# Two repeated operands of a selective scan, moved from shared tiles into tiles of their own

## The chip, the cores and the metric

The kernel runs on one core of one Trainium2 chip. The metric is the device time of one execution in microseconds (us); lower is better. All arithmetic is fp32. The core has five instruction streams that matter here: PE (matrix products), DVE (vector), ACT (activation functions), POOL (GpSimd, elementwise here) and SP, which computes nothing and issues nearly all DMAs.

## The reference, cut to what matters

The network has two layers. Layer 0 normalizes an image batch (4, 384, 32, 32) over channels, runs a selective scan over its 1024 pixels in four directions, adds the residual, and sends the tokens through a top-2-of-4 mixture of experts. Layer 1 is an attention whose query, key and value are one projection, followed by a factored feed-forward. The change lies in the scan:

```python
dts = jnp.einsum('bkrl,kdr->bkdl', dts, dt_projs_weight)
dt = jax.nn.softplus(dts + dt_projs_bias[None, :, :, None])
def step(h, inp):
    dtt, ut, bt, ct = inp
    dA = jnp.exp(dtt[..., None] * A)
    h = h * dA + (dtt * ut)[..., None] * bt[:, :, None, :]
    y = jnp.einsum('bkdn,bkn->bkd', h, ct)
    return (h, y)
```

There are 4 images, 4 directions k, 384 channels d, and 16 states n for each channel. dt and dt * u have no state axis, so a kernel that lays states on partitions has to repeat them over the states.

## The kernel before, in words

**Tiling of the scan.** A unit is one image, one direction and one half of the pixels (HF = 512); there are 4 x 4 x 2 = 32 units, in the order of `scan_layer` (L235 to L240). A unit is worked in three chunks of 128 channels (`chunk`, L373), so the scan has 96 chunks. The 128 partitions of a tile in a chunk hold 4 states x 32 channels, so a chunk needs 4 groups of states (g, NG = 4) times 4 blocks of 32 channels. The blocks are taken in two pairs: q = 0 and q = 1, each with j = 0 and 1.

**What one chunk does.** First it loads, for each q, a tile `dtr` of 128 x 2 x 2 x 512 (8 KB a partition, L382): index s = 0 is dt, s = 1 is dt * u, and each is repeated over the four states, so it is filled by eight DMAs of 128 KB out of the scratch array `dd` in HBM (L386). The pool holds three such tiles (`bufs=3`), and one chunk uses two. Then, for each g and each q:

- POOL multiplies dt * u by B into a tile `bx` of 128 x 1024 (L401; six buffers);
- ACT makes `da` = exp(A * dt) in PSUM, one instruction for each j (L410; two buffers);
- DVE runs the recurrence over 512 pixels, one `tensor_tensor_scan` for each j (L415). For q = 0 the result goes into `bx`, for q = 1 into `da`;
- the product with C is POOL's for q = 0 (L429, 128 x 1024) and DVE's for q = 1 (L422, 128 x 512, one for each j);
- PE sums over the states into `acc` (L436), which frees `bx`. After four groups DVE adds `acc` to the image's result (L276 or L280).

So a chunk holds 8 POOL products of L401 and 4 of L429, 16 exponentials, 16 scans, and 16 matmuls. In units that begin a direction, a DVE copy keeps the last column (L421, L426) as the carry for the next unit.

**What makes dt.** `project` (L287) runs for the next unit while this unit is scanned; `next(project)` (L267) advances it one step for each g. For each c of three it makes dt by softplus out of six ACT instructions (`begin`, L343 to L348), two POOL subtractions (L360, L361), two DVE instructions (L366, L367) and an ACT copy (L368), and stores dt and dt * u to `dd` (L369, L370). Its temporaries come from one tag, `k2`, of 2 KB tiles with seven buffers: `wdt` and `xd`, which live through the whole of `project`, and for each c `mag`, `one_e` and `lnw`. `mag` and `one_e` are what the stores read, so their buffers come free when the stores have landed. `k2` also serves the squares of `layernorm` (L159) and the residual tiles of `finish` (L228).

**What sets the order.** Each engine and SP work through a queue of their own, in order. The order in each queue is made when the program is built, by the framework's scheduler, out of a timing model of its own; buffers are handed out there too, so a change of tile sizes can move instructions on every queue. `issue_after` (L351) keeps the POOL and DVE steps of `project` behind named steps of the chunk.

**What runs beside the scan.** The later stages of image b (routing, experts, attention and feed-forward, called the tail here) are worked beside the scan of the images after it; the experts' weights come in 576 KB DMAs on the same SP queue (L740, L748). The last image's experts, attention and feed-forward come after the end of the scan. Attention loads its projection weights in four pieces of 128 columns into the tag `got` (L863, 1.5 KB), which has two buffers in the room `NARROW` (the tail beside the scan) and three in `WIDE` (the last image).

Of the kernel before, what the change touches and what calls it, by code (L numbers as in the profile page):

```python
# [9 lines left out]
F32 = mybir.dt.float32  # L10
I32 = mybir.dt.int32
AF = mybir.ActivationFunctionType
# [5 lines left out]
P = 128  # L18
# [5 lines left out]
HF = 512  # L24
# [20 lines left out]
DB = 32  # L45
NB = D // DB
NJ = P // DB
# [21 lines left out]

NARROW = {"kw": 8, "k12": 2, "k4": 4, "got": 2, "bb": 2}
WIDE = {"kw": 11, "k12": 3, "k4": 4, "got": 3, "bb": 2}
EXACT = {"kw": 4, "k12": 2, "k4": 4, "got": 2}

# [33 lines left out]
class Body:  # L109
# [34 lines left out]
    def layernorm(self, src, dst, eps, psum, work):  # L144

        nc = self.nc
        for i in range(NH):
            sl = halves(i)
            mean = psum.tile([P, HF], F32, tag="ps", name="ln_mean")
            for c in range(DC):  # L150
                nc.tensor.matmul(mean, self.ones, src[:, c, sl], start=(c == 0), stop=(c == DC - 1))
            for c in range(DC):
                nc.vector.scalar_tensor_tensor(
                    dst[:, c, sl], mean, -1.0 / D, src[:, c, sl], op0=ALU.mult, op1=ALU.add
                )

            sqs = []
            for c in range(DC):
                sq = work.tile([P, HF], F32, tag="k2", name="ln_sq", bufs=7)  # L159
                nc.scalar.activation(sq, dst[:, c, sl], AF.Square)  # L160
                sqs.append(sq)
            nm = HF // P
            var = psum.tile([P, HF], F32, tag="ps", name="ln_var")
            for m in range(nm):
                for c in range(DC):
                    nc.tensor.matmul(
                        var[:, m : m + 1], sqs[c][:, m * P : (m + 1) * P], self.ones[:, :1],
                        start=(c == 0), stop=(c == DC - 1),
                    )
            std = work.tile([P, nm], F32, tag="ln_std", name="ln_std", bufs=2)  # L170
            self.exp_again(
                nc.scalar.activation(std, var[:, :nm], AF.Sqrt, bias=eps, scale=1.0 / D).ins
            )
            nc.vector.reciprocal(std, std)
            rows = psum.tile([P, HF], F32, tag="ps", name="ln_rows")
            for m in range(nm):
                nc.tensor.matmul(
                    rows[:, m * P : (m + 1) * P], std[:, m : m + 1].to_broadcast([P, P]),
                    self.ident, start=True, stop=True,
                )  # L180
            for c in range(DC):
                nc.vector.tensor_mul(dst[:, c, sl], dst[:, c, sl], rows)
# [3 lines left out]
    def scan_layer(self, x1, between):  # L186

        nc, tc, a = self.nc, self.tc, self.a
        with ExitStack() as ctx:
            wp = ctx.enter_context(tc.tile_pool(name="s_w", bufs=1))  # L190
            work = ctx.enter_context(tc.tile_pool(name="s_work", bufs=1))
# [6 lines left out]
            nega = wp.tile([P, KG * NB * NG], F32, tag="nega", name="nega")  # L198
# [20 lines left out]
            def finish(b, y):  # L219
                self.layernorm(y, y, self.eps5, psum, work)  # L220
                for c in range(DC):
                    ins = nc.scalar.activation(
                        y[:, c, :], y[:, c, :], AF.Gelu,
                        bias=self.col("lnb", c), scale=self.col("lnw", c),
                    ).ins
                    rows = slice(c * P, (c + 1) * P)
                    for i in range(NH):
                        x = work.tile([P, HF], F32, tag="k2", name="x", bufs=7)  # L228
                        nc.sync.dma_start(out=x, in_=a["x"][b][rows, halves(i)])
                        nc.gpsimd.tensor_add(x, x, y[:, c, halves(i)])  # L230
                        nc.sync.dma_start(out=x1[b][rows, halves(i)], in_=x)
                self.exp_again(ins)
# [15 lines left out]
            for n, unit in enumerate(units):  # L248
# [13 lines left out]
                for c in range(DC):  # L262
# [5 lines left out]
                    if k % 2 == 0:  # L268
                        ys = y[:, c, halves(i)]
                        out = acc  # L270
# [16 lines left out]
    def project(self, unit, u, wx, work, dram, psum, made):  # L287

        nc, a = self.nc, self.a
        b, k, i = unit
        by_cols = k % 2 == 1
        w = slice(i * (HW // NH), (i + 1) * (HW // NH))

        def part(c):
            if by_cols:
                return u[:, c, :].rearrange("p (h w) -> p w h", h=HW)[:, w, :]
            return u[:, c, halves(i)]  # L300

        def split(ap):
            return ap.rearrange("p (w h) -> p w h", h=HW) if by_cols else ap

        def k2(name, shape=(P, HF)):
            return work.tile([*shape], F32, tag="k2", name=name, bufs=7)

        wdt = k2("wdt", (R, D))
        nc.sync.dma_start(out=wdt, in_=a["wdt"][:, k, :])
        ps = psum.tile([P, HF], F32, tag="ps", name="xd_ps")  # L310
        for c in range(DC):
            nc.tensor.matmul(  # L312
                split(ps[:XD, :]), wx[:, c, k, :], part(c), start=(c == 0), stop=(c == DC - 1)
            )
        xd = k2("xd", (XD, HF))
        nc.scalar.copy(xd, ps[:XD, :])
        rows = dram.tile([2 * NS, HF], F32, tag="rows", name="rows")
        nc.sync.dma_start(out=rows, in_=xd[R:XD, :])
        view = rows.rearrange("(t g n) l -> n t g l", t=2, g=NG)
        bcs = []  # L320
        for h in range(NG // 2):
            bc = work.tile([P, 2, 2, HF], F32, tag="bcs", name="bcs", bufs=3)
            for n in range(NJ):
                for t in range(2):
                    nc.sync.dma_start(
                        out=bc[n * DB : (n + 1) * DB, t],
                        in_=view[n, t, 2 * h : 2 * h + 2].partition_broadcast(DB),
                    )
            bcs.append(bc)

        dd = dram.tile([2, D, HF], F32, tag="dd", name="dd")
        made += [bcs, dd]
        yield

        def begin(c):
            ps = psum.tile([P, HF], F32, tag="ps", name="dt_ps")
            nc.tensor.matmul(ps, wdt[:, c * P : (c + 1) * P], xd[:R, :], start=True, stop=True)  # L340
            bias = self.col("dtb", k * DC + c)
            mag, one_e, lnw = k2("mag"), k2("one_e"), k2("lnw")
            nc.scalar.activation(mag, ps, AF.Abs, bias=bias)  # L343
            nc.scalar.activation(ps, ps, AF.Relu, bias=bias)
            nc.scalar.activation(mag, mag, AF.Exp, scale=-1.0)
            nc.scalar.activation(one_e, mag, AF.Identity, bias=1.0)
            nc.scalar.activation(lnw, one_e, AF.Ln)
            nc.scalar.activation(one_e, one_e, AF.Identity, bias=self.minus1)  # L348
            return ps, mag, one_e, lnw

        def behind(engine):  # L351
            if self.place_behind is None:
                return nullcontext()
            return self.tc.issue_after(self.place_behind[engine])

        for c in range(DC):
            ps, mag, one_e, lnw = begin(c)
            yield
            with behind("pool"):
                nc.gpsimd.tensor_sub(mag, one_e, mag)  # L360
                nc.gpsimd.tensor_sub(lnw, lnw, mag)  # L361
            yield
            d, du = mag, one_e
            rows = slice(c * P, (c + 1) * P)
            with behind("dve"):
                nc.vector.tensor_add(ps, ps, lnw)  # L366
                nc.vector.tensor_mul(split(du), split(ps), part(c))  # L367
            nc.scalar.copy(d, ps)  # L368
            nc.sync.dma_start(out=dd[0, rows, :], in_=d)  # L369
            ins = nc.sync.dma_start(out=dd[1, rows, :], in_=du).ins  # L370
        made.append(ins)

    def chunk(self, unit, first, c, fed, carry, nega, sel, acc, work, dap):  # L373
# [5 lines left out]
        bcs, dd, _ = fed  # L379
        dtr = []  # L380
        for q in range(NJ // 2):
            t = work.tile([P, 2, 2, HF], F32, tag="dtr", name="dtr", bufs=3)  # L382
            at = c * P + q * 2 * DB
            for n in range(NJ):
                for s in range(2):
                    nc.sync.dma_start(  # L386
                        out=t[n * DB : (n + 1) * DB, s],
                        in_=dd[s, at : at + 2 * DB, :].rearrange("(j d) l -> d j l", d=DB),
                    )
            dtr.append(t)  # L390

        def run(ap):
            return ap[:, ::-1] if k >= 2 else ap
# [2 lines left out]
        for g in range(NG):  # L396
            bc = bcs[g // 2]
            out = []
            for q in range(NJ // 2):
                bx = work.tile([P, 2, HF], F32, tag="bx", name="bx", bufs=6)  # L400
                pool = nc.gpsimd.tensor_mul(  # L401
                    bx, dtr[q][:, 1], bc[:, 0, g % 2].unsqueeze(1).to_broadcast([P, 2, HF])
                ).ins
                cg = bc[:, 1, g % 2]
                at = ((c * 2 + q) * NG + g) * 2
                for j in range(2):
# [1 line left out]
                    col = (k * NB + block) * NG + g  # L408
                    da = dap.tile([P, HF], F32, tag="da", name="da")
                    nc.scalar.activation(  # L410
                        da, dtr[q][:, 0, j, :], AF.Exp, scale=nega[:, col : col + 1]
                    )
                    hold = carry[:, at + j : at + j + 1]
                    h = bx[:, j, :] if q == 0 else da
# [877 lines left out]
```

## Time and profile before

| | |
|---|---|
| median of 3 runs | 4843.51 us (4836.32 to 4863.11) |
| profiled execution | 4820.35 us, its span 4816.9 us |
| POOL busy | 3095.1 us (64%) |
| DVE busy | 3038.3 us (63%) |
| PE busy | 3556.8 us (74%) |
| ACT busy | 2563.6 us (53%) |
| mean granted TensorE clock | 0.813 |

The span is the time between the first and the last instruction of the profiled execution; the 3.45 us between it and the execution's own time lie around the program. Busy shares are means over the whole span, and the kernel has two stages: the scan, up to about 3617 us, and what is left of the last image's tail, to the end. In the stretch from 60 to 1000 us POOL is busy for 855.04 of 940 us, from 2000 to 3000 us for 834.19 of 1000 us, and from 3615 us on for 66.74 of 1202 us. A busy share of a stage is therefore what to read, then the idle time of the engine that is fullest there, and what ended it. In the answers about waits, "A <- B: t, n" means that engine A sat idle for t us in all, n times, before the instruction named first, until the one named after the arrow was done.

### The profile page before, as it was taken

What the parts mean: (1) busy time and instruction counts of PE and PEld (TensorE: products, weight loads), DVE (VectorE), ACT (ScalarE), POOL (GpSimd) and SP (SyncE); (2) the same over time, 40 slices, a digit from 0 to 9 for tenths busy, and PEclk for the clock granted to TensorE, in tenths of its full rate; (3) what the DMA queues carried; (4) which work ended last, traced back from release to release, by engine and by line L of the source; (5) the groups of instructions that cost most, each with busy time, mean ns of one, the idle gap of its engine ahead of it and who ended that gap; (6) DMA issues with size and microseconds to landing.
All of it is one profiled execution on the core that took longest, in us unless ns stands there. A gap on an engine that the chain in (4) does not pass through costs nothing. (4 is left out here: it accounts for less than half of the span.)

```text
span 4816.9 us, 46613 instructions
## 1 busy us (share of the span) xinstructions
PE 3556.8 (74%) x13984; PEld 1713.4 (36%) x13984; DVE 3038.3 (63%) x4276; ACT 2563.6 (53%) x4390; POOL 3095.1 (64%) x1515
## 2 busy tenths in 40 slices
PE   4333334479996787566999868865789999998797
PEld 1000002245552222223556512222457665554323
DVE  5888886767778776987877788898772020002101
ACT  4454444455665666464666677655554243343454
POOL 5999997688888678778886889987880110001000
PEclk6555555589997888777999889876899999999797
DMA  4454463388777334346787754434965663332000
GB/s 110 110 118 106 110 159 92 99 238 223 216 221 203 98 96 121 80 131 189 221 242 213 197 144 102 121 88 120 262 181 185 202 226 105 125 105 91 15 15 14
DMA packets 402884, 685.56 MB, mean 142 GB/s; under 512 B 50496, under 2 KB 203456, under 8 KB 402624
## 3 DMA queue, kind: packets, MB, share of 16 engines
q1 hardware_dynamic: 393888, 656.94, 49.2%
q0 software_dynamic: 8192, 25.17, 1.6%
q8 instruction: 112, 1.84, 0.2%
q14 instruction: 148, 1.21, 0.1%
q10 hardware_dynamic: 544, 0.40, 0.0%
HBM read 557.53 MB, written 124.78 MB: 142 GB/s over the span
## 5 line engine op out<-in xcount | busy, mean ns | idle before, releaser
L401 POOL TENSOR_TENSOR bx<-dtr,bcs 128x1024 f32<-128x1024 f32 x768 | 1798.1, 2364 | 287.4 <-PE acc L436 150.9
L410 ACT ACTIVATE da<-dtr,nega 128x512 f32<-128x512 f32 x1536 | 1041.9, 689 | 1172.7 <-DVE bx L422 688.8
L429 POOL TENSOR_TENSOR bx<-bx,bcs 128x1024 f32<-128x1024 f32 x384 | 904.2, 2356 | 156.3 <-DVE carry L426 69.8
L436 PE MATMUL acc<-bx,sel 128*32 128x512 f32 x3072 | 563.9, 770 | 594.0 <-POOL bx L429 468.6
L786 PE MATMUL h_ps<-xc,w 128*128 128x256 f32 x3168 | 770.4, 397 | 67.5 <-DVE xc L770 32.4
L802 PE MATMUL y_ps<-w,hs 128*128 128x384 f32 x2112 | 741.0, 503 | 35.9 <-ACT hs L795 32.0
L786 PEld LDWEIGHTS h_ps<-xc,w 128*128 128x128 f32 x3168 | 614.5, 198 | 269.7 <-issue 97.5
L415 DVE TENSOR_TENSOR_SCAN bx<-da,carry,bx 128x512 f32<-128x512 f32 x384 | 473.9, 1269 | 122.1 <-POOL bx L401 69.8
L802 PEld LDWEIGHTS y_ps<-w,hs 128*128 128x128 f32 x2112 | 404.9, 195 | 368.0 <-issue 85.6
L415 DVE TENSOR_TENSOR_SCAN da<-da,carry,bx 128x512 f32<-128x512 f32 x384 | 475.9, 1273 | 89.5 <-ACT da L410 51.7
L415 DVE TENSOR_TENSOR_SCAN bx<-da,bx 128x512 f32<-128x512 f32 x384 | 453.6, 1210 | 100.4 <-POOL bx L401 62.1
L415 DVE TENSOR_TENSOR_SCAN da<-da,bx 128x512 f32<-128x512 f32 x384 | 454.7, 1218 | 95.5 <-POOL bx L401 53.0
L422 DVE TENSOR_TENSOR bx<-da,bcs 128x512 f32<-128x512 f32 x768 | 507.4, 678 | 2.2
L820 POOL DMA_INDIRECT got<-made,g_pos x64 | 60.7, 948 | 656.6 <-PE s_ps L894 506.1
L899 ACT ACTIVATE ex<-s_ps 128x512 f32<-128x512 f32 x512 | 299.2, 590 | 318.8 <-PE s_ps L894 318.2
L436 PEld LDWEIGHTS acc<-bx,sel 128*32 128x32 f32 x3072 | 76.5, 120 | 967.3 <-POOL bx L429 654.1
L894 PE MATMUL s_ps<-w 64*128 64x512 f32 x1024 | 312.2, 680 | 95.3 <-ACT ex L899 95.2
L791 ACT ACTIVATE hs<-h_ps,bb 128x256 f32<-128x256 f32 x528 | 210.8, 470 | 208.5 <-PE h_ps L786 208.4
L806 DVE TENSOR_TENSOR y<-y_ps,bb 128x384 f32<-128x384 f32 x88 | 48.4, 550 | 427.6 <-PE y_ps L802 426.5
L943 PE MATMUL o_acc<-ex,vt 128*64 128x512 f32 x1024 | 301.1, 667 | 0.0
L340 PE MATMUL dt_ps<-xd,wdt 12*128 12x512 f32 x192 | 141.0, 822 | 66.7 <-ACT mag L368 47.3
L312 PE MATMUL xd_ps<-u,wx 128*44 128x512 f32 x192 | 143.1, 894 | 61.4 <-ACT mag L368 61.4
(182 smaller groups left out, 3743.9 us busy)
## 6 DMA issues: line engine op xcount, KB each, us to landing
w<-in_w SPq DMA_DIRECT2D x352, 576.0 KB
dtr<-dd SPq DMA_DIRECT2D x1536, 128.0 KB
bcs<-rows SPq DMA_DIRECT2D x512, 128.0 KB
dd<-one_e SPq DMA_DIRECT2D x96, 256.0 KB
dd<-mag SPq DMA_DIRECT2D x96, 256.0 KB
rows<-zero SPq DMA_DIRECT2D x88, 192.0 KB
xs<-rows SPq DMA_DIRECT2D x44, 384.0 KB
made<-y SPq DMA_DIRECT2D x44, 384.0 KB
```

Source lines behind the costliest of these rows:

```text
L401: pool = nc.gpsimd.tensor_mul(bx, dtr[q][:, 1], bc[:, 0, g % 2].unsqueeze(1).to_broadcast([P, 2, HF])).ins
L410: nc.scalar.activation(da, dtr[q][:, 0, j, :], AF.Exp, scale=nega[:, col : col + 1])
L415: nc.vector.tensor_tensor_scan(run(h), run(da), run(bx[:, j, :]), 0.0 if first else hold, ALU.mult, ALU.add,)
L422: dve = nc.vector.tensor_mul(bx[:, j, :], h, cg).ins
L429: pool = nc.gpsimd.tensor_mul(bx, bx, cg.unsqueeze(1).to_broadcast([P, 2, HF])).ins
L436: nc.tensor.matmul(acc[lo : lo + DB, :], sel, out[q][:, j, :], start=(g == 0), stop=(g == NG - 1),)
L786: nc.tensor.matmul(ps[:, r, :], w1[(f + r) // wf][:, c, (f + r) % wf * P : ((f + r) % wf + 1) * P], xc[:, c, :], start=(c == 0), stop=(c = ...
L791: nc.scalar.activation(hs[:, f + r, :], ps[:, r, :], AF.Identity, bias=bb[:, f + r : f + r + 1])
L802: nc.tensor.matmul(out[:, :D], hs[:, f, t * P : (t + 1) * P], w2[f // wf][:, f % wf, :], start=(f == 0), stop=(f == FC - 1),)
L894: nc.tensor.matmul(ps[:, o, :], w[rows, j * P : (j + 1) * P], w[rows, halves(i)], start=True, stop=True,)
L899: ins = nc.scalar.activation(ex[:, o, :], ps[:, o, :], AF.Exp, scale=HD**-0.5, accum_out=sums[:, t, 2 * j + o, i : i + 1],).ins
L943: ins = nc.tensor.matmul(out[cols, :], made[t][1][:, j, cols], ex[:, o, :], start=(j == 0), stop=(j == MB - 1),).ins
```

## The change

`dtr` is split: dt and dt * u of one pair q go into two tiles of 128 x 2 x 512 (4 KB a partition) instead of the two halves of one tile of 8 KB. There are seven buffers of 4 KB instead of three of 8 KB: 28 KB instead of 24 KB a partition. The loops over s and n change places, so that the four DMAs of dt are issued before the four of dt * u; their number, sizes and contents stay. Room for the added 4 KB comes from `k2`, six buffers instead of seven (2 KB less), and from `got` in `NARROW`, one instead of two (1.5 KB less). The operations on the data are the same.

```diff
-NARROW = {"kw": 8, "k12": 2, "k4": 4, "got": 2, "bb": 2}
+NARROW = {"kw": 8, "k12": 2, "k4": 4, "got": 1, "bb": 2}
...
-                sq = work.tile([P, HF], F32, tag="k2", name="ln_sq", bufs=7)
+                sq = work.tile([P, HF], F32, tag="k2", name="ln_sq", bufs=6)
...
-                        x = work.tile([P, HF], F32, tag="k2", name="x", bufs=7)
+                        x = work.tile([P, HF], F32, tag="k2", name="x", bufs=6)
...
-            return work.tile([*shape], F32, tag="k2", name=name, bufs=7)
+            return work.tile([*shape], F32, tag="k2", name=name, bufs=6)
...
         for q in range(NJ // 2):
-            t = work.tile([P, 2, 2, HF], F32, tag="dtr", name="dtr", bufs=3)
+
+            pair = []
             at = c * P + q * 2 * DB
-            for n in range(NJ):
-                for s in range(2):
+            for s in range(2):
+                t = work.tile([P, 2, HF], F32, tag="dtr", name="dtr", bufs=7)
+                for n in range(NJ):
                     nc.sync.dma_start(
-                        out=t[n * DB : (n + 1) * DB, s],
+                        out=t[n * DB : (n + 1) * DB],
                         in_=dd[s, at : at + 2 * DB, :].rearrange("(j d) l -> d j l", d=DB),
                     )
-            dtr.append(t)
+                pair.append(t)
+            dtr.append(pair)
...
-                    bx, dtr[q][:, 1], bc[:, 0, g % 2].unsqueeze(1).to_broadcast([P, 2, HF])
+                    bx, dtr[q][1], bc[:, 0, g % 2].unsqueeze(1).to_broadcast([P, 2, HF])
...
-                        da, dtr[q][:, 0, j, :], AF.Exp, scale=nega[:, col : col + 1]
+                        da, dtr[q][0][:, j, :], AF.Exp, scale=nega[:, col : col + 1]
```

Below, L388, L404, L413, L432 and L439 of the kernel after are L386, L401, L410, L429 and L436 of the kernel before; lines up to L370 keep their numbers, and lines from L405 on are three higher.

## The prediction

> **What bounds the kernel now.** I read the stretches first. After 3615 us the scan is over, PE is busy 1088.51 of 1202 us, and the change reaches nothing there directly. Before that no engine is full all the time, so I read the idle time of the fullest one, POOL.
>
> ```profile
> POOL bx L401 <- PE acc L436: 150.9, 28, 35.7
> POOL bx L401 <- DMA dtr<-dd: 113.8, 41, 9.5
> POOL bx L429 <- DVE carry L426: 69.8, 26, 6.6
> POOL mag L360 <- ACT one_e L348: 69.7, 15, 44.4
> POOL bx L429 <- DVE bx L415: 46.9, 23, 3.9
> ```
>
> These are POOL's waits (total us, times, longest us). The second is what the change is about: 113.8 us before L401 until a DMA of `dtr` had landed. One wait of 9.5 us is the start, which stays; 104.3 us in 40 waits are left, 2.6 us each.
>
> The rows by line give POOL's work: L401 768 x 2.364 us, L429 384 x 2.356 us, L360 and L361 96 x (1.272 + 1.275) us. A chunk is 8 x 2.364 + 4 x 2.356 + 2.55 = 30.9 us. The times of the DVE adds that end chunks (L276, L280) show the pace: from 344.79 to 525.65 us six chunks end, 30.1 us each (records of neighbouring instructions overlap a little), so POOL is solid there. With the tail beside the scan, from 828.33 to 3617.39 us, 72 chunks take 38.7 us each: 8 us a chunk lie in a tangle of waits, and the waits for `dtr` are 1.4 us of it (98.8 us of the 104.3 fall here).
>
> Then SP, which issues the loads:
>
> ```profile
> SPq L386 <- ACT da L410: 414.5, 67, 34.9
> ...
> SPq L370 <- DVE one_e L367: 316.1, 54, 21.9
> ...
> SPq L386 <- POOL bx L401: 41.5, 24, 17.8
> ```
>
> A pair's tile is free only when both POOL (dt * u) and ACT (dt) have read it for the last time; ACT is the later one ten times as often by time. ACT is tied to DVE by two `da` buffers:
>
> ```profile
> ACT da L410 <- DVE bx L422: 688.8, 356, 8.8
> ```
>
> POOL runs ahead of both, so it reaches the next chunk's second pair while ACT still holds the tile that this pair's data needs. The order of time shows it, for instance, where three L401 in a row start at 1128.09 after 7.83 us of idle time, released by a load.
>
> **What the Trainium skill says.** "Perfetto Trace Analysis", section Optimization Strategy: the same gap coming again on the engine that should be full can mean that there is no room for the next tile. The trace agrees: 40 gaps, mostly at the second pair of a chunk. "PSUM — Partial Sum Buffer", section Engine vs sequencer instructions: the queues of ScalarE, VectorE and GpSimdE are strictly first in, first out, so an ACT instruction that waits for a store holds the exponentials behind it. Beyond that principle no trace here has such a wait in number. "DMA: Bandwidth & Descriptors", section Anatomy of one DMA, fits 2.0 us plus bytes / 436 GB/s, for the GpSimd path: an estimate of 2.6 us for a 256 KB store. The trace has more on the SP path: a store issued at 50.69 us released ACT at 54.70 us, 4.0 us. I use 4.0.
>
> **The change part by part**, against the profiled 4820.35 us (span 4816.9 + 3.45 around it). The median, 4843.51, is 23.2 us (0.5%) above it; I add the same differences to both.
>
> *1. Seven tiles for three pairs: gain.* A chunk needs four tiles, so three of the next chunk's four can be in place before any tile comes free: both of the first pair, and dt of the second. Only the second pair's dt * u waits for a buffer, and that is the one POOL itself gives back at its last L401 of q = 0, not ACT. At 260 to 280 us, POOL's last such read ends at 268.1 us and ACT's at 269.8; and after it only four issues (about 0.46 us each: 16 took 7.36 us), not eight, have to go out. So it lands about 1.7 + 1.8 = 3.5 us earlier than now. That covers most of 2.6 us a wait; the longest (7.8 us) stay in part. The number of loads is the same (1536 x 128 KB), so SP and HBM do no less work. What is late next: POOL's products with C (L429), which wait for DVE (69.8 + 46.9 us now), because with a busy DVE (80% from 2000 to 3000 us) an earlier `bx` just lies longer. Hence only a share of 104.3 us reaches the end. Bounds: 0 (all handed on) to -104 us; I take half, **-52 us**. The swap of the loops lets ACT start after four loads instead of seven of eight, which helps ACT's 99.5 us of waits for `dtr`; POOL still needs the last of eight. I count it within the half.
>
> *2. The order moves.* In the built program's order, PE has 2885 matmuls after the last `acc` matmul instead of 2951: 66 fewer, half an expert's slot. From 3615 us on PE takes 1088.51 / 4387 = 0.248 us each, so 16 us; they go into the scan, where PE is busy for 80 to 83% and delays `acc` in turn. Bounds 0 to -16; I take **-8 us**. In the first image POOL's order was two products of L401 to one of L429; now it is mostly six, then three. Over three groups POOL needs 23 us, DVE 3 x 6.3 + 1.8 = 20.7 us; but the third L429 waits for five half groups of scans that begin behind the first L401, 16.9 us, against 16.2 to 17.5 us of POOL's own queue. Before, four POOL products (9.4 us) lay between the first product of a group and its L429, against 2.5 us of scans. So DVE's slack falls from about 7 us to under 1 us. At 0 to 1 us for each of some 30 such bursts: 0 to +30, I take **+8 us**. The later images have about the old mixture.
>
> *3. Six `k2` instead of seven: loss.* `wdt` and `xd` hold two, so four are left for three temporaries; the next `lnw` (L347) needs a buffer that a store of the channel block before still reads. In the order of ACT's waits, 83 of 96 L347 now wait for a DMA, where 4 did; of L343 70, where 30 did; L346 falls from 40 to 6. Queued behind on ACT are the exponentials, for which DVE waits, and for DVE POOL's L429. How long a wait is depends on the exponentials between the copy L368 and the wait: with two or fewer (55 waits) 4.0 us of landing against 2 x 0.69 us at the least leaves up to 2.6 us. A `da` that is ready ahead covers about one scan, 1.25 us. Upper bound: 55 x 1.35 = 74 us. But before, 22 such short waits stood in the order, and the trace shows one hold of 2.9 us. Bounds 0 to +74, I take **+10 us**. `layernorm` and `finish` use six at most; hidden.
>
> *4. One `got` instead of two.* A later piece's load can still be issued a whole piece early. Only the second of an image waits for the first's matmuls, in three images; 192 KB land in about 4 us. Cover is the attention's other work. Bounds 0 to +12, I take **+3 us**.
>
> Sum: -52 - 8 + 8 + 10 + 3 = **-39 us**: 4781 profiled, 4804.5 against the median, which I round to **4805 us**, 0.8% faster.
>
> **Rivals.**
>
> *The gap is handed on.* All 104 us of `dtr` turn into waits for DVE and `acc`, and the small terms cancel. For it: POOL's waits for DVE are as large as those for `dtr`, and the stage beside the tail is bound by no single engine. Against it: where POOL runs free it does keep its pace. About 4840 us, within 0.5% (24 us).
>
> *Slower: ACT holds behind the stores.* The dd stores stand in SP's queue among loads that wait for buffers (414.5 us now), so a store is late, L347 holds ACT, DVE starves, and POOL, with the bunched order, has no slack. At term 3's upper end: +74, with a quarter of the gain (-26), +8, +3, -8: +51 us, 4895 us. It decides from about 0.9 us lost on DVE at each of 55 waits (49 us, what the other terms give at half gain), or 0.4 us at a quarter. For it: 159 waits of `begin` for DMAs instead of 74. Against it: the old 74 cost 2.9 us in all.
>
> *The change doesn't do what it says*, because SP is blocked by an expert's weights (L748 <- PE 373.1 + 259.6 us) when the buffer comes free: the gain goes, and the order alone decides, 4843 + 13 = 4856 us at terms 2 to 4 as taken. I count it with the other two.
>
> **How the numbers follow.** Faster, at half gain: 0.43. Handed on, within 0.5%: 0.20. Slower (ACT's holds, or SP's block with them): 0.37. 0.5% (24 us) is about what a measurement of this kernel can tell from no change. The likeliest case's own range is 4725 (gain 104, tail 16, nothing lost) to 4819 us. The range of 8 in 10 leaves out the tip of the first and what lies beyond the second rival: 4740 to 4900 us.
>
> **What would show it.** Right: POOL's wait of L401 for `dtr` falls from 113.8 to under 50 us, SP's loads wait for POOL as often as for ACT, and the last L439 ends 30 to 50 us earlier than 3617 us. Term 3 shows as waits of ACT's L343 and L347 for `dd`: under 30 us as I take it, over 100 us in the slower case, with DVE's waits for `da` (L415 <- ACT, 172.7 us now) grown by half as much. The bunched order shows as a pace above 30.5 us a chunk in the first image. I am wrong if `dtr` waits fall and the scan still doesn't end earlier, and the reason then stands among POOL's waits for DVE and `acc`.

## The result and the profile after

The kernel after takes 4800.23 us (median of 6 runs, 4793.39 to 4808.13), the kernel before 4853.84 us (6 runs, 4836.32 to 4863.11): a ratio of 0.9893, 95% interval 0.9870 to 0.9915, 52 us less. A repeat on another occasion gave 0.9907 (0.9885 to 0.9930), 45 us less. So the change makes the kernel faster by about 1%, where -39 us was forecast. The profiled execution of after took 4793.39 us, its span is 4791.8 us. The profile of before comes from an execution of 4820.35 us, faster than any of its six runs here, so this pair of profiles is only 27 us apart.

POOL's waits in the kernel after (total us, times, longest us), to be held against the first fence of the prediction:

```profile
POOL bx L404 <- PE acc L439: 159.7, 33, 44.3
POOL bx L432 <- DVE bx L418: 113.5, 43, 7.8
...
POOL mag L360 <- ACT one_e L348: 88.9, 13, 43.8
...
POOL bx L432 <- DVE carry L429: 48.7, 25, 10.0
POOL bx L404 <- DMA dtr<-dd: 33.9, 10, 7.4
```

The wait for `dtr` went from 113.8 us in 41 waits to 33.9 us in 10, as the change means it to. But L432, the product with C, now waits 113.5 us for DVE's scans, where L429 waited 46.9 us before. POOL's idle time has mostly moved to other waits: these five groups sum to 451.1 us before and 444.7 us now. What SP's loads of `dtr` wait for, in the same kernel:

```profile
SPq L388 <- ACT da L413: 434.5, 98, 29.1
...
SPq L388 <- POOL bx L404: 152.0, 48, 15.2
```

The tile of dt * u is now given back by POOL alone, and the loads that wait for POOL have grown (41.5 us before, 152.0 now). The loads that wait for ACT do so about as long as before (414.5 us, now 434.5); they are dt's.

The stretch behind the end of the scan, first of the kernel before, then of the kernel after (us; PE, PE's weight loads, DVE, ACT, POOL busy with their counts; TensorE clock, DMA share, GB/s):

```profile
3617.00:4817.00 1200.00, 1086.51 (x4370) 605.74 (x4366) 157.01 (x329) 492.35 (x952) 66.45 (x56) 0.94 0.33 108
```

```profile
3614.00:4792.00 1178.00, 1056.83 (x4244) 579.56 (x4240) 151.78 (x326) 482.91 (x937) 66.61 (x56) 0.93 0.32 106
```

The scan ends at 3614.4 us instead of 3617.4, only 3 us earlier. 22 us of the 25 between the two spans lie in the stretch of which the prediction says that "the change reaches nothing there directly": PE has 126 records less there and is busy for 29.7 us less. In a second pair of profiles, both from one chip (c0 and c3 below), the scan ends at 3641.6 us before and 3625.6 us after, 16 us earlier, and the rest takes 1211.2 and 1183.4 us, 28 us less. The end of the scan differs between single profiles of one kernel by 11 to 24 us, so I take times from the runs and only the counts and the kind of waiting from the profiles.

### The profile page after: what moved, and what is told of

It is laid out like the page before. It is cut to its first block, busy times and chain, and to the rows that moved or that the text cites. A ratio compares the mean times of both kernels' runs of the same rounds, so it can differ in the third digit from the quotient of the medians.

```text
span 4791.8 us, 46970 instructions
## 1 busy us (share of the span) xinstructions
PE 3529.4 (74%) x13984; PEld 1709.7 (36%) x13984; DVE 3018.9 (63%) x4276; ACT 2568.3 (54%) x4390; POOL 3096.8 (65%) x1515
## 4 chain that ended last, share of the span: by engine, by line
PE 32%; DVE 18%; ACT 8%; issue 6%; DMA 4%; POOL 3%; SPq 2%; another core or an unknown queue 0%; DVEq 0%; POOLq 0%; ACTq 0%
PE y_ps L805 8%; PE h_ps L789 8%; DVE da L418 5%; DVE bx L418 5%; PE s_ps L897 3%; PE o_acc L946 3%; DVE bx L425 2%; ACT da L413 2%; POOL bx L404 2%; PE o_ps L993 1%; PE acc L439 1%; PE w_ps L874 1%; DMA dtr<-dd 1%; PE xd_ps L312 1%; ACT hs L798 1%
## 5 line engine op out<-in xcount | busy, mean ns | idle before, releaser
L404 POOL TENSOR_TENSOR bx<-dtr,bcs 128x1024 f32<-128x1024 f32 x768 | 1800.2, 2379 | 200.3 <-PE acc L439 159.7
L413 ACT ACTIVATE da<-dtr,nega 128x512 f32<-128x512 f32 x1536 | 1044.6, 690 | 1130.8 <-DVE bx L425 658.1
L432 POOL TENSOR_TENSOR bx<-bx,bcs 128x1024 f32<-128x1024 f32 x384 | 906.8, 2372 | 202.8 <-DVE bx L418 113.5
L439 PE MATMUL acc<-bx,sel 128*32 128x512 f32 x3072 | 557.1, 755 | 582.1 <-POOL bx L432 429.5
L789 PE MATMUL h_ps<-xc,w 128*128 128x256 f32 x3168 | 771.7, 397 | 57.7 <-DVE xc L773 30.3
L789 PEld LDWEIGHTS h_ps<-xc,w 128*128 128x128 f32 x3168 | 614.1, 198 | 266.9 <-issue 100.8
L439 PEld LDWEIGHTS acc<-bx,sel 128*32 128x32 f32 x3072 | 83.1, 121 | 949.3 <-POOL bx L432 581.7
```

The source lines that it names most:

```text
L404: pool = nc.gpsimd.tensor_mul(bx, dtr[q][1], bc[:, 0, g % 2].unsqueeze(1).to_broadcast([P, 2, HF])).ins
L413: nc.scalar.activation(da, dtr[q][0][:, j, :], AF.Exp, scale=nega[:, col : col + 1])
L432: pool = nc.gpsimd.tensor_mul(bx, bx, cg.unsqueeze(1).to_broadcast([P, 2, HF])).ins
L439: nc.tensor.matmul(acc[lo : lo + DB, :], sel, out[q][:, j, :], start=(g == 0), stop=(g == NG - 1),)
L789: nc.tensor.matmul(ps[:, r, :], w1[(f + r) // wf][:, c, (f + r) % wf * P : ((f + r) % wf + 1) * P], xc[:, c, :], start=(c == 0), stop=(c = ...
```

## The experiments

My theory was that of the prediction: the waits for `dtr` were the gain. The rivals were that the gain comes from the reordered queues (a slot, 256 tokens that one expert works on, moved out of the last stretch), and that the waits are handed on. In the table, "us" is (ratio - 1) times the median of before that was measured on the same chip; "moved" is how many of PE's matmuls stand behind the last `acc` matmul in the built program, fewer than in before; PE's records in the traces give the same counts. The runs come from several chips, on which before takes from 4827 to 4854 us, so between rows from different chips it is the ratios that can be compared; medians and single profiles differ there by up to 0.5% from the chip alone.

| run | median us | ratio (95%) | us | moved |
|---|---|---|---|---|
| after, first measurement | 4800.23 | 0.9893 (0.9870 to 0.9915) | -52 | 66 |
| c0_before_again | 4856.23 (one run) | | | 0 |
| c1_split_six | 4835.37 | 0.9966 (0.9952 to 0.9980) | -16 | 45 |
| c2_less_room | 4830.72 | 0.9957 (0.9941 to 0.9974) | -21 | 52 |
| c3_after_again | 4811.01 | 0.9907 (0.9885 to 0.9930) | -45 | 66 |
| d1_after_six_tiles | 4809.53 | 0.9956 (0.9944 to 0.9968) | -21 | 30 |
| d2_few_loads | 4758.96 | 0.9845 (0.9831 to 0.9860) | -75 | 117 |
| d3_before_experts_early | 4856.81 | 1.0053 (1.0037 to 1.0069) | +26 | 174 |
| d4_after_experts_early | 4830.93 | 1.0005 (0.9995 to 1.0015) | +2 | 277 |
| e1_after_experts_held | 4807.62 | 0.9954 (0.9936 to 0.9972) | -22 | 24 |
| e2_less_room_held | 4821.44 | 0.9986 (0.9979 to 0.9994) | -7 | 24 |
| e3_k2_five_held | 4881.57 | 1.0109 (1.0088 to 1.0129) | +53 | 24 |
| f1_even_products | 4782.45 | 0.9868 (0.9849 to 0.9888) | -64 | 31 |

### The parts by themselves: c0, c1, c2, c3

c0 and c3 are before and after again. c1 has the split, but not its price in room: six tiles of 4 KB (the same 24 KB), `k2` and `got` as before. c2 pays the price (one `k2` and one `got` buffer less) and has no split.

```diff
 c1, against after
-NARROW = {... "got": 1, ...}            k2: bufs=6      dtr: bufs=7
+NARROW = {... "got": 2, ...}            k2: bufs=7      dtr: bufs=6
 c2, against before
-NARROW = {... "got": 2, ...}            k2: bufs=7
+NARROW = {... "got": 1, ...}            k2: bufs=6
```

> The kernel before once more, unchanged, for a second profile of it. The two profiles so far put the end of the scan at 3617.4 us before and 3614.4 us after, and the stretch behind it at 1199.5 and 1177.4 us: of 25 us of span, 22 lie behind the scan. If that split is the change's own, this profile repeats 3617 and 1200 us within about 5 us each. If the scan's length varies between executions by 10 us or more, the split of one pair of profiles says little.

> The split alone, with six tiles of 4 KB in the room of the three of 8 KB, and k2 and got as before. Theory A (the gain is POOL's removed wait for dt * u, in the scan): dt * u is given back by POOL alone here too, so the wait for dtr falls from 114 us to about 70 and the scan ends about 15 us earlier; ratio about 0.996. Theory B (the gain is expert work that the new order puts into the scan): the order here has 45 fewer matmuls behind the last acc matmul than before, 45 x 0.248 = 11 us; the stretch behind the scan gets shorter by that and the scan does not; ratio about 0.998. Theory C (the seventh tile and the split are needed together): no gain, 1.000.

> The price alone: k2 with six buffers and got with one, dtr in three tiles of 8 KB as before. Theory A: no gain and the loss of term 3, ACT holding behind stores, 0 to 20 us; ratio 1.000 to 1.004. Theory B: the order has 52 fewer matmuls behind the last acc matmul than before (13 us), so the stretch behind the scan gets shorter by about 13 us with dtr's waits unchanged near 114 us; ratio about 0.997.

> The kernel after once more, unchanged. The ratio repeats, 0.989 within 0.003. Theory A: the scan ends earlier than that of the kernel before on the same chip by about 30 us. Theory B: the scan ends within 10 us of it, and the stretch behind it is about 20 us shorter.

Measured: the split with six tiles gives -16 us, the price alone gives a *gain* of 21 us, and both with the seventh tile -45 us. POOL's wait for `dtr` in c1:

```profile
POOL bx L404 <- DMA dtr<-dd: 109.6, 40, 9.1
```

The split alone leaves the waits where they were (113.8 and 121.2 us in the two profiles of before). d1 below shows that it is the seventh tile that takes them away. That fewer buffers made the kernel faster by themselves (c2) speaks against theory A of its expectation and for theory B, which expected 13 us; it called for another look at term 2.

### Is it the seventh tile, and what are the remaining waits worth: d1, d2

```diff
 d1, against after
-  name="dtr", bufs=7
+  name="dtr", bufs=6
 d2, against after
+        if c > 0:
+            dtr = self.kept
-        for q in range(NJ // 2):
+        for q in range(NJ // 2 if c == 0 else 0):
...
+        self.kept = dtr
```

> The kernel after with six dtr tiles instead of seven (k2 six, got one, split as after): the seventh tile alone is taken away. Theory A (the removed wait in the scan is a real part of the gain): the wait of POOL's first product for dtr comes back to about 110 us from 35, as in the split with six tiles, and 20 to 30 us of the gain are lost; ratio about 0.996. Theory B (only expert work moved ahead of the scan's end counts): 30 fewer matmuls lie behind the last acc matmul than before, a quarter of an expert's slot of 33 us, so 8 us are gained; ratio about 0.998. Both see a loss against after; the difference is in the waits and in where the scan ends.

> The kernel after, which loads dt and dt * u only for the first of a unit's three chunks and uses these tiles for all three: two thirds of the loads are left out, and the two other chunks compute with the first one's values. No wait for dtr can be left but the first. Theory A at half gain: the last 30 us of waits and the SP and DMA time go, the scan gets 20 to 40 us shorter than that of after; ratio about 0.982. Theory 'handed on': the scan ends where after's ends, within 10 us, and POOL's second product waits longer for DVE; the order has 51 matmuls fewer behind the scan than after, 13 us; ratio about 0.987.

With six tiles -21 us: what the price alone gives. Most of POOL's waits for `dtr` are back:

```profile
POOL bx L404 <- DMA dtr<-dd: 82.0, 28, 6.3
```

d2 leaves out two thirds of the loads: all three chunks of a unit compute with the values of the first, so its result is not the network's and it serves as a probe only. The wait for `dtr` is 14.8 us, and the kernel is faster than before by 75 us, 30 us more than the repeat of after. POOL's waits in that kernel:

```profile
POOL bx L407 <- PE acc L442: 168.2, 37, 52.0
...
POOL bx L435 <- DVE bx L421: 76.8, 35, 8.2
...
POOL bx L435 <- DVE carry L432: 68.1, 27, 7.1
...
POOL bx L407 <- DMA dtr<-dd: 14.8, 6, 4.1
```

POOL still waits for DVE and PE, no less than before (313.1 us in the first three groups, 267.6 us in before). In the profile the scan ends at 3624.1 us, no earlier than in after; the rest takes 1137.8 us, 40 us less than in after, with 51 matmuls less behind the scan. Both point to the experts' work.

### The experts' work moved on purpose: d3, d4

The same edit on before and on after: the experts of every image get a higher priority with the scheduler.

```diff
-        self.experts(b, routed, room)
+        with self.tc.high_priority(offset=1000):
+            self.experts(b, routed, room)
```

> The kernel before, with the experts given a somewhat higher priority in the scheduler; no tile, buffer or operation is changed. The order of POOL in the first three images is as before; 174 fewer matmuls lie behind the last acc matmul, 1.4 slots of an expert. Theory B: 1.4 x 33 = 46 us are cut behind the scan, and the scan gets longer by a part of it, since PE's acc matmuls queue behind them; if half is given back, -23 us, ratio about 0.995. Theory A: moving PE work doesn't help, since the scan is bound by POOL and DVE waits that PE's queue makes worse; ratio 1.000 or above, with dtr's waits unchanged near 115 us.

> The kernel after, with the same higher priority for the experts: 211 fewer matmuls behind the last acc matmul than after, 1.7 slots (55 us), of which half is given back in the scan. Theory B: another -25 us; ratio to before about 0.985. Theory A: no further gain, 0.989 to 0.993. If both hold side by side, the gains add: 0.985.

The stretch behind the scan gets shorter: 1166.8 us (from 1199.5) and 1100.9 us (from 1177.4). But the scan ends at 3683.2 and 3725.1 us, 66 and 111 us later, and both kernels lose: d3 as theory A said, d4 more than any theory said. A slot is 66 matmuls. So work cannot be moved out of the last stretch into the scan without limit: moving 2.6 slots costs more than it gives, 4.2 slots undo the change's whole gain. (The edit reorders the other engines too.) These runs show that the place of the experts' work matters, not what 66 matmuls are worth.

### The experts' work held back: e1, e2, e3

So I took the move away instead. In the third image, whose experts still run at the end of the scan, the first matmuls of the slots from number 5 on (counted from 0) go behind the last `acc` matmul in PE's queue. 24 matmuls are then moved instead of 66 (e1, on after) and instead of 52 (e2, on the price alone). The third run, e3, is e1 with `k2` cut once more, to five buffers.

```diff
+                    self.last_acc = nc.tensor.matmul(acc, ...).ins
...
+    def held(self, b, s):
+        if b == B - 2 and s >= 5:
+            return self.tc.issue_after(self.last_acc)
+        return nullcontext()
...
+                        with self.held(b, s):
                             nc.tensor.matmul(h_ps, ...)
```

> The kernel after, in which the first products of the experts' slots 5 and later of the third image stand on PE behind the scan's last acc matmul, so that the amount of expert work behind the scan is as in the kernel before to within half a slot (24 matmuls fewer), while the scan's own order is that of after. Theory W (the removed waits are real scan time, which after gives out as expert work done beside the scan): without that work the scan ends 30 to 45 us earlier than that of before, at about 3595 us, the stretch behind it takes about 1195 us, and the ratio stays at 0.988 to 0.991. Theory O (the waits for dtr are handed on to DVE, and after's gain is only the moved slot): the scan still ends at 3615 to 3625 us and the ratio goes up to 0.995 to 0.998.

> The price alone (k2 six, got one, dtr as before) with the same hold on the experts' slots, so with the same expert work behind the scan as the run before. Theory W with the prediction's term 3 (six k2 cost ACT a little): the scan is no shorter than before's, and the 0.996 of the unheld version goes; ratio 1.000 to 1.003. Theory O (what counts is moved work): ratio 0.998, from the 24 matmuls. Theory K (six k2 make the scan itself shorter): the ratio stays at about 0.996 and the scan ends some 15 us earlier than before's.

> The held version of after with k2 cut once more, to five buffers: two for wdt and xd, three for mag, one_e and lnw, so that each of begin's three temporaries waits for a store of the channel block before (87 of L346 and 80 of L347 wait for a DMA in the order). Term 3 as predicted (ACT holds behind stores, and DVE starves): 20 to 60 us slower than the held version with six, ACT's waits for dd above 100 us. If store waits are covered by the exponentials that stand between, less than 10 us slower, with ACT's waits for dd under 30 us.

On after, holding back 42 matmuls costs 23 us (-45 to -22; 30 us against the first measurement), on the price alone 28 matmuls cost 14 us (-21 to -7): 0.5 to 0.7 us a matmul. The numbers are those of theory O in the expectations. The prediction took 0.248 us a matmul. The page of after shows why that is too little:

```profile
L439 PE MATMUL acc<-bx,sel 128*32 128x512 f32 x3072 | 557.1, 755 | 582.1 <-POOL bx L432 429.5
```

The program issues 16 `acc` matmuls in each of 96 chunks, 1536; the profile counts 3072. Each of these matmuls is two records, and so are the experts' products with their weights (L789: 3168 records for 44 slots of 36). Only the six transposes of a slot (L770) are one record each: 264 records for 44 slots. A slot's 66 matmuls are 60 products and 6 transposes, 126 records: exactly what was missing behind the scan, and at 0.248 us a record 31 us, not 16. Where nothing else comes between, the adds that end a slot stand 33.9 us apart in the second profile of before (3826.77 and 3860.63 us); other slots there take up to 61 us.

The profiles don't confirm this price. The stretch behind the scan in c3, where 66 matmuls are moved, and in e1, where 24 are:

```profile
3626.00:4809.00 1183.00, 1062.72 (x4240) 586.48 (x4238) 151.16 (x325) 481.53 (x937) 66.48 (x56) 0.92 0.32 105
```

```profile
3626.00:4809.00 1183.00, 1074.84 (x4319) 597.95 (x4318) 155.71 (x326) 488.60 (x950) 66.53 (x56) 0.93 0.32 106
```

PE has 79 records more in e1's stretch (78 of them are the held matmuls') and is busy for 12 us longer, but idle for as much less: the stretch is as long. The same holds for c2 and e2 (1178.9 and 1179.2 us). e1's and e2's chip is faster by 0.5%, which makes up for 6 us. So the price of a held matmul rests on the medians of the runs alone, and where the held kernels lose their time stays open. The order of POOL's instructions in e1 is that of after, but for one.

What is left is 15 us between e1 and e2 (0.9954 and 0.9986, the same hold on the same chip): that is all that the split with the seventh tile brought in after as it was built, though its waits for `dtr` are just as small (37.1 us) in e1.

With five `k2` buffers the kernel loses 75 us against e1. The cause is not ACT held behind stores: ACT waits 15.3 us (before `lnw`) and 8.5 us (before `one_e`) for `dd`. The third image takes 1017.8 us in the profile instead of 961.8. Near its end stands POOL's longest wait of that image, 33.02 us in e1 and here 53.58 us; POOL's timeline with five buffers:

```profile
2681.95 13.95 POOL L404 TENSOR_TENSOR bx<-dtr,bcs 128x1024 f32<-128x1024 f32 x6 [53.58 <-PE acc L439]
```

In those microseconds the layernorm of the fourth image runs, in two halves one after the other, and the scan stands still. `k2` also serves `layernorm` (L159), so a shortage there fits; it is not shown, since the two halves follow one another in e1 too. So going from seven `k2` buffers to six is cheap, from six to five it is not, and the loss is not in the place that the prediction feared. The longer wait is 20 us of the 75; where the rest arises stays open.

### The bunches taken away: f1

Why do the vanished waits bring so little? POOL's timeline of after, in the first image and in a later one (start, us, instruction, idle time before it):

```profile
299.73 13.94 POOL L404 TENSOR_TENSOR bx<-dtr,bcs 128x1024 f32<-128x1024 f32 x6
313.56 2.41 POOL L432 TENSOR_TENSOR bx<-bx,bcs 128x1024 f32<-128x1024 f32 x1
315.87 1.34 POOL L360 TENSOR_TENSOR mag<-one_e,mag 128x512 f32<-128x512 f32 x1
317.09 4.73 POOL L432 TENSOR_TENSOR bx<-bx,bcs 128x1024 f32<-128x1024 f32 x2
...
2863.48 2.36 POOL L432 TENSOR_TENSOR bx<-bx,bcs 128x1024 f32<-128x1024 f32 x1 [5.70 <-DVE bx L418]
2869.97 2.36 POOL L432 TENSOR_TENSOR bx<-bx,bcs 128x1024 f32<-128x1024 f32 x1 [4.13 <-DVE bx L418]
2875.58 11.61 POOL L404 TENSOR_TENSOR bx<-dtr,bcs 128x1024 f32<-128x1024 f32 x5 [3.25 <-PE acc L439]
```

In the first image six products with B go ahead of three with C, as the prediction said, and there is no idle time. In a later image the same habit may do harm: the L432s stand alone in POOL's queue and wait for a scan each, and products with B come only afterwards, in a bunch of five. (That they could have filled those gaps isn't shown: the first of them waits for `acc` itself.) Along POOL's timeline, with L360 and L361 passed over, after has 86 bunches of four or more L404, 30 of them in the first image; before has 31, one of them in the first image. Both kernels with six tiles have before's pattern (30 and 35 bunches, one or two of them in the first image). So the bunches come with the seventh tile. The edit keeps L404 of a group behind the L432 of the group two before, in POOL's queue, which still allows four in a row; the data and buffers are those of after, and nothing is held back on PE. Of bunches of five or more after has 52, before 12, f1 one.

```diff
+            behind = self.products[-2] if len(self.products) > 1 else None
...
+                with self.tc.issue_after(behind) if behind is not None else nullcontext():
                     pool = nc.gpsimd.tensor_mul(bx, dtr[q][1], ...).ins
...
+                    self.products.append(pool)
```

> The kernel after, with one thing added to POOL's order: the products with B of a group stand behind the product with C of the group two before (as they mostly did in the kernel before), so POOL's bunches of six and three are gone; run-ahead is 4 or less throughout. Expert work behind the scan is 35 matmuls more than in after and 31 fewer than in before, close to the held version (0.9954). If the bunches make POOL's L432 wait for DVE (110 us in after, 47 before), these waits fall back to about 50 us and the ratio is below the held version's, 0.988 to 0.992. If L432's waits are the dtr waits handed on, because DVE is late whatever POOL's order, they stay near 110 us, or turn up before L404, and the ratio is 0.994 to 0.998.

Measured: 0.9868, -64 us, the fastest kernel of the study, with only 31 matmuls moved. The stretch behind its scan, and POOL's waits:

```profile
3592.00:4781.00 1189.00, 1073.51 (x4308) 597.23 (x4304) 152.18 (x326) 489.53 (x950) 66.52 (x56) 0.93 0.32 106
```

```profile
POOL bx L407 <- PE acc L443: 137.9, 29, 35.0
...
POOL bx L435 <- DVE bx L421: 67.2, 34, 6.3
POOL bx L435 <- DVE carry L432: 65.5, 32, 5.6
...
POOL bx L407 <- DMA dtr<-dd: 45.1, 15, 9.3
```

The product with C (L435 here) waits 67.2 us for the scans instead of 113.5, but 65.5 us for the copies of the carry instead of 48.7: together 132.7 us instead of 162.2. `dtr` stays low at 45.1 us. The scan ends at 3592.3 us, 22 us before that of after, while the rest is 11 us longer, since 35 of the 66 matmuls are back there: here the gain lies in the scan, as the prediction wanted it.

That these shorter waits are the gain is not shown. By the adds that end a chunk, the four images' scans take 822, 951, 962 and 880 us in after and 820, 919, 950 and 904 us here: most of the gain is in the second image, and the fourth loses. In the second image POOL's waits for DVE before the product with C are as long as in after (33.4 and 31.0 us). What shrank there is its wait for `acc` before the product with B (37.8 us instead of 74.2), and PE has 112 records less in that image (2836 instead of 2948) and 112 more in the third. So the one constraint has also moved tail work from one image to the next.

The same profile has ACT waiting 36.2 us before `lnw` for stores, more than ACT waits for stores of `dd` in any other kernel here (after 6.2, d2 15.6, e3 23.8 us), and the kernel is the fastest all the same.

## Why the prediction was right, point by point

The runs can be put into a sum, if the terms simply add and one matmul moved is worth 0.5 us throughout (two records of 0.248 us). From e2: -7 us = -12 for 24 matmuls **+5 for the price**. From f1: -64 = -15.5 for 31 matmuls + 5 **- 53 for the tiles**. From e1: -22 = -12 + 5 - 53 **+ 38 for the bunches**. Then after should be -33 (66 matmuls) + 5 - 53 + 38 = -43 us; -45 and -52 were measured. The price alone should be -26 + 5 = -21, measured -21. Neither is a test, since both runs had a part in finding the 0.5 us. Few loads is one: -58 + 5 - 15 (the tiles and the bunches together) = -68, measured -75. So this is an account, not a proof: the last two terms are remainders, "tiles" holds all else that f1's constraint brought and "bunches" all else in which e1 differs from f1, and each term carries 10 to 15 us from the intervals.

**1. The waits for `dtr`: right about the waits, not shown in size.** The sign that was named came: under 50 us left (33.9). In after as built, the split with the seventh tile and the bunches brought 15 us together (e1 against e2), where -52 + 8 = -44 us was forecast for them; the -53 of the sum equals the forecast -52 only if f1's constraint brought nothing else. SP's loads wait for POOL more, but not as often as for ACT (48 times against 98), and the scan did not end 30 to 50 us earlier. The prediction didn't say that the split alone would do nothing: by the sum it is worth +6 us with six tiles (c1: -16 = -22 + 6) or -11 us (d1: -21 = -15 + 5 - 11). The Trainium skill, "Perfetto Trace Analysis", section Optimization Strategy, says that a gap which keeps repeating on the engine that should be full can mean too little room for the next tile. The runs agree: with one more tile the waits shrink to a third (33.9 us), with the same room cut in halves they stay (109.6 us).

**2. The order moves: the step that failed, twice, in opposite directions.** "66 fewer, half an expert's slot, ... 16 us; ... I take -8" was a whole slot, 31 us by its 126 records, and worth -33 us by the sum. The term was mis-sized because a program's count was multiplied by a duration per record, and because half was then taken off for what the scan would pay. "0 to +30, I take +8" for the bunches was +38 by the sum, as a remainder. The place was wrong as well: a pace above 30.5 us in the first image was to show them, but six chunks there take 182.1 us, 30.35 each (30.1 before). The scan of the first image even ends about 6 us earlier in after (822.4 us, before 829.0; 824.3 and 829.9 in the second pair). In the later images, where I wrote "about the old mixture", after has 56 bunches of four or more against 30, and POOL's waits before L432 grew there. Why the bunches cost time, if they do, is not shown. As the two errors nearly cancel (-33 + 38 against -8 + 8), that the forecast's sum came out right was in this part luck.

**3 and 4. Six `k2`, one `got`: right in kind.** +13 together was forecast, and the sum gives +5. ACT's waits for stores of `dd` sum to 6.2 us in after:

```profile
ACT da L413 <- DMA dtr<-dd: 29.8, 20, 3.8
...
ACT lnw L347 <- DMA dd<-one_e: 6.2, 3, 3.2
```

Under 30 us, as taken. (The prediction's remark that no trace had such a wait in number is at odds with its own term 3, which names one of 2.9 us in before.) Most of the 83 waits of L347 that the order shows find the store landed: only three cost time. DVE's waits for `da` grew from 172.7 to 195.9 us (114.4 + 81.5), which is no sign of the slower case without ACT being held. With one `got` alone the built order of PE, ACT, DVE and POOL is that of before, line for line; on SP's queue only the loads of these weights stand later, by one piece. Term 4 was not run by itself.

**The rivals.** *Handed on* describes after's scan better than my likeliest case: the waits for `dtr` fell by 80 us, those for the scans before L432 grew by 67 us, and the scan ended 3 us (or 16) earlier, not 30 to 50. By the prediction's own test (waits down, scan no earlier) that comes close to wrong. The kernel was faster all the same, and by the counts the slot that left the last stretch is 31 of the 45 to 52 us; f1 shows that with another order the scan does end earlier with the same tiles. *Slower, ACT holds* is refuted: even at five `k2` buffers ACT's waits for stores are 24 us, and at 36.2 us (f1) the kernel is the fastest. *Doesn't do what it says* is refuted by the waits.

**Open.** How much of f1's gain is POOL's order itself and how much the other queues, which the scheduler also reorders when one constraint is added, isn't told apart: in the traces PE, DVE and ACT too stand in another order in f1 than in after, while e1 leaves nearly everything in place. Nor is it known where the 75 us at five `k2` buffers arise. That -33 us comes from 66 moved matmuls rests on a slope from two pairs (42 and 28 matmuls) whose profiles don't show it in the last stretch. It cannot hold without limit: with 174 moved the kernel is slower (d3).

## What to carry to other kernels

When one tile has two readers on different engines, split it by reader and add room for at least one more piece: here the split alone left the waits at 110 us, and the seventh piece took them to 34 us. Shorter waits are not yet time: as built, this brought about 15 us. After any change of buffers compare the built order of every queue before you believe in the local mechanism: here a slot moved between stages was by its records worth 31 us, where 39 were forecast for everything together, and an ordering constraint on one instruction (f1) made the fastest kernel of the study. Before multiplying a program's count by a duration from the trace, divide the trace's count of a known line by the program's.

## What was not expected of the hardware

Two records for each fp32 product that was counted, but one for a transpose: 3072 for the 1536 `acc` matmuls, 264 for the 264 transposes of L770; on average 0.248 us a record and so 0.5 us a matmul of two records in the last stretch. Beyond that nothing; single profiles of one kernel ended their scan 11 to 24 us apart (3617.4 and 3641.6 us before; 3614.4 and 3625.6 us after), as much as the terms in dispute, so that only the runs could decide.
